# Layer 1's 8-bit product moved by tiles into its attention, and wider products for the absorbed weights

## The chip, the core and the metric

The kernel runs on one core of a Trainium2 chip. The metric is the device time of one execution in microseconds (us), as a median over several runs. The core has a matrix engine (TensorE, PE in the profile; PEld is its loading of the stationary operand), VectorE (DVE), ScalarE (ACT), GpSimd (POOL), and SyncE (SP), which here only issues transfers (DMAs). Each engine executes its own instructions in order and waits for the others through semaphores. PE writes its products to PSUM; DVE and ACT copy them from there to SBUF.

## The reference, cut to what matters

Four layers over x (16 sequences of 56 tokens, width 256), each an attention over a context of 1500 positions and a feed-forward part. Layers 1 to 3 have a latent attention with 16 heads; layers 0, 2 and 3 end in experts with a router, layer 1 in one product with 8-bit weights and inputs that are rounded to 8 bits.

```python
# attention of layers 1 to 3 (layer 2 also ropes q_big)
q_hk = (hidden_q @ Wq.T).reshape(b, s, H, K)
q_big = einsum('bshk,hkq->bshq', q_hk, w_kc_q)
q_r = einsum('bshq,hqr->bhsr', q_big, W_qr)
k_r = einsum('bld,hdr->bhlr', kv_rope, W_kr)
attn = softmax(einsum('bhsr,bhlr->bhsl', q_r, k_r))
ctx_c = einsum('bhsl,bld->bhsd', attn, kv_rope)
ctx_lat = einsum('bhsd,hkd->bshk', ctx_c, w_kc_kv)
out = ctx_lat.reshape(b, s, H * K) @ Wo.T
# feed-forward part of layer 1
w = weight.astype(f32) * weight_scale
x_fp8 = clip(x / input_scale, -448, 448).astype(float8_e4m3fn)
out = einsum('bsi,oi->bso', x_fp8.astype(f32) * input_scale, w)
# each layer
x = x + tanh(g_xattn[l]) * attention(layernorm(x))
x = x + tanh(g_ffn[l]) * feed_forward(layernorm(x))
```

## The kernel before

The tokens stay in SBUF as eight tiles of 112 rows (`x`, two sequences each). Instructions are traced in the order of the Python code; a scheduler may move them on their engine, except that `in_order` pins an instruction behind the one traced before it on the same engine. Nearly all of the steps here are pinned, the queries (L346, L337) are not.

**Absorbing.** The weights of the latent attention do not depend on tokens, so for each group `g` of two heads `absorbing` multiplies them into two matrices: `M`, which turns a normalized token into the two heads' queries against the latent context, and `G`, which turns the heads' contexts into the output. Layers 1 and 3 have three products in a chain, with a copy out of PSUM behind each: W_qr times W_kr (L280, `e`), w_kc_q times `e` (L288, `f`), Wq times `f` (L297, `M`), and w_kc_kv times Wo (L304, `G`). Layer 2 ropes between, so it keeps two factors: `M` of 384 columns (L258, L259) and `er` (L265, copied by L267 and, under a mask by `C_H`, by L269). `load_heads` fetches a group's six weights over SP's queue (L231), two buffers to a weight. Some groups are absorbed ahead of a layer (`Next.absorb`; several at once take turns), the others within `queries`.

**Queries.** For layers 1 and 3, `queries` computes all queries of a group in two halves of 448 tokens (L337), and `spread` copies each with DVE (L316) and ACT (L318); the next group's absorption is traced between. Layer 2 has three products (L346), the roping (L350, L353, and L354 on POOL), and two products more (L360, L362).

**Attention.** `attention_mla` goes through 56 steps, seven to a tile of tokens, each 128 queries of two sequences. In loop turn `k`, step `k` gets its scores (PE, L711), maxima (DVE, L723 to L728) and exponentials (ACT, L734, L743), step `k - 1` has its probabilities turned (PE, L773) and copied (DVE L776, ACT L778), and step `k - 2` multiplies them with the context (PE, L785) and keeps the result (DVE, L796). The sums of the exponentials are inverted and go through memory to all partitions (`invert`, SP, L760 and L762). In layer 1 the next tile's keys are turned in three of the steps (L696). When a tile's seven steps are done, `project(t)` multiplies its contexts by `G` (L808) and adds to `x` (L810), as a generator of which `next(after)` traces one part at a time, at three places of each turn: one behind the first maxima, two behind the exponentials. In layers 2 and 3 the router's work on that tile follows in the same generator (L922 to L1015).

**The 8-bit product.** `fp8_matrix` loads the 8-bit weights (three DMAs on SP) and decodes them on DVE by integer operations (L1450 to L1464), between layer 1's queries and its attention. `fp8_linear` runs behind the attention, with two tiles at a time: statistics, ACT's square root (L172), normalizing, rounding to 8 bits in float32 (L1479 to L1485), turning (L189, L190), two products to a tile (L1494), the addition to `x` (L1499), then the normalization of the result and its turning to `xnT`, the input of layer 2's queries. Four absorptions of layer 2 are traced in between.

The main program's order for layer 1:

```python
    with tc.tile_pool(name="f1w", bufs=1, reuse_waits="tile") as keep:
        matrix = []
        attention_mla(1, nxt, behind_queries=lambda: matrix.extend(fp8_matrix(keep)))
        nxt.whole.close()
        nxt = Next(2)
        fp8_linear(*matrix, nxt)
```

## Time and profile before

| | us |
|---|---|
| median of 3 runs | 2435.41 |
| lowest and highest run | 2428.84, 2443.81 |
| profiled execution | 2433.22 |
| its span, of which the profile's times are told | 2431.4 |

Where the span goes, by stretches of the trace:

| stretch (us from the start) | what | PE busy | granted PE clock |
|---|---|---|---|
| 0 to 310.5 | layer 0 | 244.4 | 0.87 |
| 310.5 to 338 | two absorptions of layer 1, layer 0's sums | 25.9 | 0.72 |
| 338 to 391 | layer 1's queries | 48.7 | 0.97 |
| 394.5 to 914.5 | layer 1's attention | 513.9 | 0.98 |
| 914.5 to 955.6 | the 8-bit product, four absorptions of layer 2 | 33.0 | 0.75 |
| 955.6 to 1076 | layer 2's queries | 117.2 | 1.00 |
| 1076 to 1598 | layer 2's attention | 512.8 | 0.99 |
| 1598 to 1688 | layer 2's experts, three absorptions of layer 3 | 80.3 | 0.83 |
| 1688 to 1736 | layer 3's queries | 45.0 | 1.00 |
| 1736 to 2258 | layer 3's attention | 515.0 | 0.99 |
| 2258 to 2431 | layer 3's experts, output | 135.6 | 0.93 |

How to read the profile: its page gives busy times and, in 40 slices of the span, tenths of each engine's busy share and of the PE clock that was granted. A row of the timeline has the start, the duration, the engine, the line of the kernel, the operation, output and inputs by the program's names, and in brackets how long the engine stood idle before it and what ended that. Rows of a window table have the stretch, its length, each engine's busy time with its number of instructions, then the granted clock, the DMA engines' busy share and GB/s. A row of waits has the waiting engine and line, what it waited for, the total, how often, and the longest. A float32 product appears as two records on PE, a transpose as one.

### The profile page before, as it was taken

How to read it: one execution, taken by the hardware profiler on the slowest of the kernel's cores; microseconds unless marked ns; L12 is line 12 of the kernel's file. 1: busy time of each engine (PE TensorE's matmuls, PEld its weight loads, DVE VectorE, ACT ScalarE, POOL GpSimd, SP SyncE). 2: the span in 40 equal slices, each digit the busy share in tenths (PEclk: the TensorE clock that was granted, in tenths of full speed). 3: DMA queues.
4: the chain of work that ended last, by engine and by line, in shares of the span. 5: the costliest groups of instructions: out<-in, count | busy, mean ns of one | idle time of the engine just before them, and what ended most of it. 6: DMA issues, size and time to landing. Idle time of an engine off the chain costs nothing. (4 is left out here: it accounts for less than half of the span.)

```text
span 2431.4 us, 48119 instructions
## 1 busy us (share of the span) xinstructions
PE 2273.1 (93%) x18034; PEld 1648.4 (68%) x18034; DVE 1507.5 (62%) x3384; ACT 1234.8 (51%) x2705; POOL 411.8 (17%) x707
## 2 busy tenths in 40 slices
PE   8678988999999998989999999979899999999687
PEld 5445665777777776447777777755577777777454
DVE  4752335667666667767777777724477777777222
ACT  4312325666666662346666666612566666665231
POOL 4454810000000001430000000001001111111223
PEclk9769988999999998999999999989899999999899
DMA  7736742000000002100000000045200000000497
GB/s 215 220 97 183 222 132 75 22 22 22 21 21 22 22 23 61 35 28 22 22 24 23 24 24 23 11 153 166 61 22 16 27 26 28 28 29 17 151 282 207
DMA packets 114115, 171.93 MB, mean 71 GB/s; under 512 B 20154, under 2 KB 75971, under 8 KB 112852
## 3 DMA queue, kind: packets, MB, share of 16 engines
q1 hardware_dynamic: 104342, 150.30, 20.4%
q0 software_dynamic: 7600, 17.14, 2.2%
q8 instruction: 145, 2.38, 0.4%
q10 hardware_dynamic: 1934, 1.34, 0.2%
q14 instruction: 94, 0.77, 0.1%
HBM read 130.19 MB, written 40.48 MB: 70 GB/s over the span
## 5 line engine op out<-in xcount | busy, mean ns | idle before, releaser
L734 ACT ACTIVATE p<-s_ps,nm 128x500 f32<-128x500 f32 x504 | 335.7, 675 | 396.8 <-DVE nm L725 396.8
L723 DVE TENSOR_REDUCE part<-s_ps 128x1 f32<-128x500 f32 x504 | 340.5, 677 | 262.9 <-PE s_ps L711 262.7
L711 PE MATMUL s_ps<-kvT,qT 64*128 64x500 f32 x2016 | 484.4, 607 | 13.7 <-ACT p L734 6.3
L785 PEld LDWEIGHTS m_ps<-pT,kv 125*64 125x64 f32 x8064 | 436.7, 137 | 76.7 <-issue 69.5
L785 PE MATMUL m_ps<-pT,kv 125*64 125x128 f32 x8064 | 477.3, 275 | 2.2 <-ACT pT L778 1.7
L711 PEld LDWEIGHTS s_ps<-kvT,qT 64*128 64x128 f32 x2016 | 185.5, 189 | 198.4 <-issue 121.1
L773 PE MATMUL m_ps<-ident,p 128*125 128x128 f32 x2016 | 299.4, 283 | 0.3
L728 DVE TENSOR_REDUCE nm<-s_ps 128x1 f32<-128x1500 f32 x168 | 287.1, 1709 | 2.3 <-PE s_ps L711 2.3
L773 PEld LDWEIGHTS m_ps<-ident,p 128*125 128x125 f32 x2016 | 249.4, 188 | 36.5 <-issue 27.0
L743 ACT ACTIVATE p<-s_ps,nm 128x1500 f32<-128x1500 f32 x168 | 254.9, 1517 | 1.3 <-DVE nm L728 0.8
L773 PE MATMUL s_ps<-ident,p 128*125 128x128 f32 x2016 | 251.3, 275 | 0.0
L754 POOL TENSOR_TENSOR den<-den 128x1 f32<-128x1 f32 x168 | 33.4, 199 | 1217.7 <-ACT p L734 1217.4
L773 PEld LDWEIGHTS s_ps<-ident,p 128*125 128x125 f32 x2016 | 237.1, 190 | 0.0
L778 ACT COPY pT<-s_ps 125x512 f32<-125x512 f32 x336 | 181.2, 598 | 90.6 <-PE s_ps L773 76.7
L778 ACT COPY pT<-m_ps 125x512 f32<-125x512 f32 x336 | 185.7, 620 | 0.0
L1217 PE MATMUL gu_ps<-wgu,xT 128*128 128x448 f32 (+2 forms) x344 | 144.0, 546 | 21.2 <-DMA wgu<-in_L_wgu 14.7
L796 DVE TENSOR_TENSOR ctxT<-m_ps,rep 64x128 f32<-64x128 f32 (+1 forms) x384 | 104.4, 272 | 88.4 <-PE m_ps L785 81.6
L1222 DVE TENSOR_TENSOR act<-gu_ps,act 128x224 f32<-128x224 f32 (+2 forms) x78 | 31.2, 400 | 193.3 <-ACT act L1221 193.3
L318 ACT COPY qT<-q_ps 64x224 f32<-64x224 f32 x128 | 71.8, 561 | 109.3 <-PE q_ps L362 71.0
L776 DVE COPY pT<-m_ps 125x512 f32<-125x512 f32 x168 | 116.2, 691 | 10.0 <-PE s_ps L773 0.4
L776 DVE COPY pT<-s_ps 125x512 f32<-125x512 f32 x168 | 114.3, 680 | 0.0
L1217 PEld LDWEIGHTS gu_ps<-wgu,xT 128*128 128x128 f32 x344 | 63.9, 195 | 72.3 <-issue 31.4
(289 smaller groups left out, 2651.2 us busy)
## 6 DMA issues: line engine op xcount, KB each, us to landing
wgu<-in_L_wgu SPq DMA_DIRECT2D x36, 448.0 KB
rows<-zero SPq DMA_DIRECT2D x16, 899.5 KB
kvT<-turned_kv SPq DMA_DIRECT2D x16, 750.0 KB
wgu<-in_L_wgu SPq DMA_DIRECT2D x34, 352.0 KB
rep<-through SPq DMA_DIRECT2D x336, 32.0 KB
xrow<-rows SPq DMA_DIRECT2D x78, 128.5 KB
wgu<-in_L_wgu SPq DMA_DIRECT2D x8, 1024.0 KB
wd<-in_L_wd SPq DMA_DIRECT2D x36, 224.0 KB
```

The lines of the kernel that those rows point to most:

```text
L318: nc.scalar.copy(o, i)
L711: in_order(nc.tensor.matmul(o[:, 0 : 4 * KP], qT[64 * b : 64 * b + 64, t, j * QT : (j + 1) * QT], kvTs[t][64 * b : 64 * b + 64, z * 4 * KP ...
L723: in_order(nc.vector.tensor_reduce(self.part[:, z : z + 1], sp0[z][:, 0 : 4 * KP], AX.X, ALU.max))
L728: in_order(nc.vector.tensor_reduce(self.nm[1], sp1[:, :, 0 : 4 * KP], AX.XY, ALU.max, negate=True))
L734: in_order(nc.scalar.activation(self.p[0][:, 4 * z * KP : 4 * (z + 1) * KP], sp0[z][:, 0 : 4 * KP], AF.Exp, bias=self.nm[0], accum_out=sel ...
L743: in_order(nc.scalar.activation(self.p[1].rearrange("p (z c) -> p z c", z=3), sp1[:, :, 0 : 4 * KP], AF.Exp, bias=self.nm[1], accum_out=se ...
L773: in_order(nc.tensor.transpose(ps[:, c, :], self.p[b][:, k : k + KP], ident))
L776: in_order(nc.vector.tensor_copy(o, ps))
L778: in_order(nc.scalar.copy(o, ps))
L785: in_order(nc.tensor.matmul(self.pv[64 * b : 64 * b + 64, :], kv[:, self.t, c, b, :], self.pT[:, c, b, :], start=c == 0, stop=c == KC - 1))
L796: in_order(nc.vector.tensor_tensor(ctxs[self.t][64 * a : 64 * a + 64, b, lo - 448 * a : hi - 448 * a], self.pv[64 * b : 64 * b + 64, cols] ...
L1217: in_order(nc.tensor.matmul(ps[:, s, 0:n], xT[:, k, :], wgu[:, k, s * n : (s + 1) * n], start=k == 0, stop=k == 1))
```

## The change

The decoding becomes a generator of 14 parts; from the second turn on, two are traced at the end of each turn of layer 1's attention, the three loads with the first. `fp8_linear` becomes `fp8_tile`, for one tile, which continues `project(t)` as the router does in layers 2 and 3; a fourth `next(after)` stands at the end of each turn, behind DVE's copies. Its roots are Newton steps on DVE (`inverse_root`) where ACT's square root stood, and its turned tiles and products use the two shared PSUM banks (`misc`). The last tile's parts are what is left behind the loop: they are traced around layer 2's absorptions, taken two at a time.

In `absorbing`, layer 2 multiplies Wq by all 192 columns at once and copies `M` in two pieces; its second factor is two products over 128 rows, with the weights laid out in blocks and the mask in the weights. Layers 1 and 3 multiply in another order: W_qr with w_kc_q first, two heads in two column halves of the array, then one product over 128 rows with W_kr in diagonal blocks. The weights are laid out for this on the host, so `wqr` and `wkr` are larger.

```diff
-        room = {"wkc": 512}.get(name, size)
-        w = wpool.tile([128 if name == "wkc" else p, room], F32, tag=name, name=name)[0:p, 0:size]
+        room = {"wkc": 512, "wqr": 256}.get(name, size)
+        w = wpool.tile([128, room], F32, tag=name, name=name)[0:p, 0:size]
         w = w.rearrange("p (n a) -> p n a", n=n) if len(rest) == 1 else w.rearrange("p (n a c) -> p n a c", n=n, a=rest[0])
...
             M = pool.tile([128, 2, 3 * 128], F32, name="Mr", bufs=bufs)
             for k in range(2):
-                ps = misc()
+                ps = misc()[:, 0 : 2 * DQ].rearrange("p (j c) -> p j c", j=2)
                 for j in range(2):
-                    lhsT = wq[:, j, k * 128 : (k + 1) * 128]
-                    rest = ps[:, 256:384].rearrange("p (b j c) -> p j b c", b=2, j=2)[:, j]
-                    pin(nc.tensor.matmul(ps[:, j * 128 : (j + 1) * 128], lhsT, wkc[:, j, 0:128], start=True, stop=True))
-                    pin(nc.tensor.matmul(rest, lhsT, wkc[:, j, 128:192].rearrange("p (b c) -> p b c", b=2), start=True, stop=True))
-                pin(nc.scalar.copy(M[:, k, :], ps[:, 0:384]))
+                    pin(nc.tensor.matmul(ps[:, j, :], wq[:, j, k * 128 : (k + 1) * 128], wkc[:, j, :], start=True, stop=True))
+                pin(nc.scalar.copy(M[:, k, 0:256].rearrange("p (j c) -> p j c", j=2), ps[:, :, 0:128]))
+                rest = M[:, k, 256:384].rearrange("p (b j c) -> p j b c", b=2, j=2)
+                pin(nc.scalar.copy(rest, ps[:, :, 128:DQ].rearrange("p j (b c) -> p j b c", b=2)))
                 yield
             ps = misc()
-            for j in range(2):
-                for lhsT, o in ((wqr[:, j, :], 0), (wqr[:, 2, :], 128)):
-                    pin(nc.tensor.matmul(ps[:, o + j * DC : o + (j + 1) * DC], lhsT, wkr[:, j, :], start=True, stop=True))
+            for i in range(2):
+                pin(nc.tensor.matmul(ps[:, i * 128 : (i + 1) * 128], wqr[:, 0, i, :], wkr[:, 0, :], start=True, stop=True))
             e = pool.tile([128, 2, 128], F32, name="er", bufs=bufs)
-            pin(nc.scalar.copy(e[:, 0, :], ps[:, 0:128]))
-            for j in range(2):
-                pin(nc.scalar.activation(
-                    e[:, 1, j * DC : (j + 1) * DC], ps[:, 128 + j * DC : 128 + (j + 1) * DC], AF.Copy, scale=small[:, C_H + j : C_H + j + 1]
-                ))
+            pin(nc.scalar.copy(e.rearrange("p i c -> p (i c)"), ps[:, 0:256]))
             yield
             made[g] = M, e
         else:
             ps = misc()
-            for j in range(2):
-                for i in range(2):
-                    c = (2 * j + i) * DC
-                    pin(nc.tensor.matmul(ps[0:96, c : c + DC], wqr[:, j, i * 96 : (i + 1) * 96], wkr[:, j, :], start=True, stop=True))
-            e = pool.tile([96, 2, 2, DC], F32, name="e")
-            pin(nc.scalar.copy(e.rearrange("p j i c -> p (j i c)"), ps[0:96, 0 : 4 * DC]))
+            for i in range(2):
+                for j in range(2):
+                    pin(nc.tensor.matmul(
+                        ps[64 * j : 64 * j + 64, 0:128], wqr[:, j, i, :], wkc[:, j, i, :], start=i == 0, stop=i == 1, skip_group_check=True
+                    ))
+            e = pool.tile([128, 128], F32, name="e")
+            pin(nc.scalar.copy(e, ps[:, 0:128]))
             yield
             ps = misc()
-            for j in range(2):
-                for i in range(2):
-                    pin(nc.tensor.matmul(ps[:, j * DC : (j + 1) * DC], wkc[:, j, i, :], e[:, j, i, :], start=i == 0, stop=i == 1))
+            pin(nc.tensor.matmul(ps[:, 0 : 2 * DC], e, wkr[:, 0, :], start=True, stop=True))
             f = pool.tile([128, 2, DC], F32, name="f")
             pin(nc.vector.tensor_copy(f.rearrange("p j c -> p (j c)"), ps[:, 0 : 2 * DC]))
...
-    def attention_mla(l, nxt, router=None, behind_queries=None):
+    def attention_mla(l, nxt, router=None, behind=None, tail=None):
...
             nxt.stack.close()
-            if behind_queries:
-                behind_queries()
             for g in range(2 if l < 3 else 0):
                 load_absorbed(l + 1, g)
...
                 if router is not None:
                     yield from router.token_tile(t)
+                if tail is not None:
+                    yield from tail(t)
...
                         turn.turned(i)
+                if tail is not None:
+                    if k > 0:
+                        next(behind, None)
+                        next(behind, None)
+                    next(after, None)
                 if val and val.j == nq - 1:
                     for _ in after:
                         pass
                     after = project(val.t)
-            for _ in after:
-                pass
+            if tail is None:
+                for _ in after:
+                    pass
+            else:
+                next(after)
+                next(after)
+            return after
...
-    def fp8_matrix(keep):
-        w8 = keep.tile([128, 2, D], F32, name="w8")
-        sc = keep.tile([128, 4], F32, name="sc")
+    def fp8_matrix(w8, sc):
...
-            nc.vector.tensor_copy(wi, wb)
-            nc.vector.tensor_scalar(mag, wi, 0x7F, None, ALU.bitwise_and)
...
+            in_order(nc.vector.tensor_copy(wi, wb))
+            yield
+            in_order(nc.vector.tensor_scalar(mag, wi, 0x7F, None, ALU.bitwise_and))
+            yield
...
-            nc.vector.tensor_tensor(sc[:, 3:4], sc[:, 0:1], sc[:, 1:2], ALU.mult)
-            nc.vector.tensor_tensor(sc[:, 3:4], sc[:, 3:4], gates[:, 5:6], ALU.mult)
-        return w8, sc
-    def fp8_linear(w8, sc, nxt):
...
-            for t in range(0, NT, 2):
-                normed.stats(t)
-                normed.stats(t + 1)
-                normed.root(t)
-            nxt.absorb(0, 1)
-            for t in range(0, NT + 4, 2):
-                if t < NT:
-                    quantize(t)
-                    multiply(t)
-                if t in (2, 4):
-                    nxt.absorb(t // 2 + 1)
-                if 2 <= t < NT + 2:
-                    add(t - 2)
-                    nxt.normed.stats(t - 2)
-                    nxt.normed.stats(t - 1)
-                    nxt.normed.root(t - 2)
-                if t >= 4:
-                    nxt.normed.apply(t - 4)
-                    nxt.normed.turn(t - 4)
...
+            in_order(nc.vector.tensor_tensor(sc[:, 3:4], sc[:, 0:1], sc[:, 1:2], ALU.mult))
+            yield
+            in_order(nc.vector.tensor_tensor(sc[:, 3:4], sc[:, 3:4], gates[:, 5:6], ALU.mult))
+            yield
+    def fp8_tile(t, w8, sc, pool):
+        def stats():
+            st = pool.tile([TP, 6], F32, name="st")
+            mv = pool.tile([TP, 2], F32, name="mv")
+            in_order(nc.vector.bn_stats(st, x[:, t, :]))
+            in_order(nc.vector.bn_aggr(mv, st))
+            return mv
+        def apply(mv, rstd):
+            v = pool.tile([TP, D], F32, name="xn")
+            in_order(nc.vector.tensor_scalar(v, x[:, t, :], mv[:, 0:1], rstd, ALU.subtract, ALU.mult))
+            return v
+        def turn(v, o):
+            ps = misc()[:, 0 : 2 * TP].rearrange("p (k c) -> p k c", k=2)
+            for k in range(2):
+                in_order(nc.tensor.transpose(ps[:, k, :], v[:, k * 128 : (k + 1) * 128], ident[0:TP, 0:TP]))
+            in_order(nc.scalar.copy(o, ps))
+        yield
+        mv = stats()
+        rstd = yield from inverse_root(pool, mv[:, 1:2])
+        yield
+        v = apply(mv, rstd)
+        c = pool.tile([TP, D], F32, name="c8")
+        in_order(nc.vector.tensor_scalar(v, v, sc[0:TP, 2:3], None, ALU.mult))
+        in_order(nc.vector.tensor_scalar(v, v, 448.0, -448.0, ALU.min, ALU.max))
+        for _ in range(4):
+            yield
+        in_order(nc.vector.tensor_scalar(c.bitcast(I32), v.bitcast(I32), 0x7F800000, None, ALU.bitwise_and))
+        in_order(nc.vector.tensor_scalar(c, c, 2.0**-6, 1.5 * 2.0**20, ALU.max, ALU.mult))
+        in_order(nc.vector.tensor_tensor(v, v, c, ALU.add))
+        in_order(nc.vector.tensor_tensor(v, v, c, ALU.subtract))
+        yield
+        x8 = pool.tile([128, 2, TP], F32, name="x8T")
+        turn(v, x8)
+        for _ in range(4):
+            yield
+        ps = misc()[0:TP, 0:D]
+        for k in range(2):
+            in_order(nc.tensor.matmul(ps, x8[:, k, :], w8[:, k, :], start=k == 0, stop=k == 1))
+        yield
+        in_order(nc.vector.scalar_tensor_tensor(x[:, t, :], ps, sc[0:TP, 3:4], x[:, t, :], ALU.mult, ALU.add))
+        yield
+        yield
+        mv = stats()
+        rstd = yield from inverse_root(pool, mv[:, 1:2])
+        yield
+        v = apply(mv, rstd)
+        yield
+        turn(v, xnT[:, :, t, :])
...
-    with tc.tile_pool(name="f1w", bufs=1, reuse_waits="tile") as keep:
-        matrix = []
-        attention_mla(1, nxt, behind_queries=lambda: matrix.extend(fp8_matrix(keep)))
+    with ExitStack() as keep:
+        f1w = keep.enter_context(tc.tile_pool(name="f1w", bufs=1, reuse_waits="tile"))
+        matrix = f1w.tile([128, 2, D], F32, name="w8"), f1w.tile([128, 4], F32, name="sc")
+        parts8 = keep.enter_context(tc.tile_pool(name="f1c", bufs=1, reuse_waits="tile"))
+        left = attention_mla(1, nxt, behind=fp8_matrix(*matrix), tail=lambda t: fp8_tile(t, *matrix, parts8))
         nxt.whole.close()
         nxt = Next(2)
-        fp8_linear(*matrix, nxt)
+        nxt.absorb(0, 1)
+        for _ in range(14):
+            next(left)
+        nxt.absorb(2, 3)
+        for _ in left:
+            pass
...
-        wqr = i[p + "W_qr"].transpose(2, 0, 1)
+        wqr = i[p + "W_qr"]
         if l == 2:
-            wqr = wqr[:, :, order].reshape(64, 8, 2, DQ)
-            rest = wqr[..., 128:].reshape(64, 8, 2, 2, 32).transpose(0, 1, 3, 2, 4).reshape(64, 8, 1, 128)
-            wqr = np.concatenate([wqr[..., 0:128], rest], axis=2).reshape(64, 24, 128)
-        a[f"L{l}_wqr"] = wqr
-        a[f"L{l}_wkr"] = i[p + "W_kr"].transpose(2, 0, 1)
+            wqr = wqr[:, order, :].reshape(8, 2, DQ, 64).transpose(1, 3, 0, 2)
+            both = np.zeros((2, 64, 8, 2, 128), np.float32)
+            both[:, :, :, 0, :] = wqr[..., 0:128]
+            for j in range(2):
+                both[j, :, :, 1, :].reshape(64, 8, 2, 2, 32)[:, :, :, j, :] = wqr[j, ..., 128:].reshape(64, 8, 2, 32)
+            a[f"L{l}_wqr"] = both.reshape(128, 8, 2, 128)
+        else:
+            a[f"L{l}_wqr"] = wqr.reshape(H, 2, 96, 64).transpose(2, 0, 1, 3)
+        blocks = np.zeros((2, 64, 8, 2, 64), np.float32)
+        for j in range(2):
+            blocks[j, :, :, j, :] = i[p + "W_kr"].reshape(8, 2, 64, 64)[:, j].transpose(2, 0, 1)
+        a[f"L{l}_wkr"] = blocks.reshape(128, 8, 128)
```

## The prediction, made before the change was run

> **What bounds the kernel now.** I read the page first (shares, slices), then layer 1 in stretches, then one step of its attention in order of time, then the waits of the stretch behind it, then one group of the queries.
>
> ```profile
> PE 2273.1 (93%) x18034; PEld 1648.4 (68%) x18034; DVE 1507.5 (62%) x3384; ACT 1234.8 (51%) x2705; POOL 411.8 (17%) x707
> PEclk9769988999999998999999999989899999999899
> ```
>
> TensorE (PE) is busy 93% of the span, so a PE instruction counts unless PE is idle or slow there. Layer 1 by stretches (engine busy times, then granted clock):
>
> ```profile
> 415.00:900.00 485.00, 485.00 (x4731) 376.56 (x4730) 332.63 (x615) 309.91 (x669) 21.05 (x108) 1.00 0.06 20
> 914.50:921.20 6.70, 2.15 (x19) 1.98 (x18) 5.82 (x24) 1.26 (x6) 0.00 (x0) 0.90 0.00 0
> 921.20:931.00 9.80, 9.80 (x44) 8.20 (x44) 7.27 (x16) 3.38 (x11) 0.00 (x0) 0.50 0.22 64
> 931.00:944.00 13.00, 10.88 (x55) 8.11 (x54) 8.29 (x25) 3.62 (x10) 0.00 (x0) 0.76 0.33 103
> 944.00:955.60 11.60, 10.12 (x56) 7.92 (x56) 8.80 (x26) 3.63 (x11) 0.17 (x1) 0.87 0.48 146
> ```
>
> The attention (first row) has PE busy throughout, VectorE (DVE) 69%, ScalarE (ACT) 64%. The 8-bit product and the first absorptions of layer 2 (41.1 us, 914.5 to 955.6) have PE idle or at half clock. One step of the attention:
>
> ```profile
> 875.95 2.79 PE L711 MATMUL s_ps<-kvT,qT 64*128 64x500 f32 x12
> 877.09 0.68 DVE L723 TENSOR_REDUCE part<-s_ps 128x1 f32<-128x500 f32 x1 [1.42 <-PE s_ps L711]
> 878.66 2.84 PE L785 MATMUL m_ps<-pT,kv 125*64 125x128 f32 x48
> 879.73 0.68 ACT L734 ACTIVATE p<-s_ps,nm 128x500 f32<-128x500 f32 x1 [2.78 <-DVE nm L725]
> 881.43 0.70 PE L773 MATMUL m_ps<-ident,p 128*125 128x128 f32 x4
> 884.25 2.79 PE L711 MATMUL s_ps<-kvT,qT 64*128 64x500 f32 x12
> ```
>
> A step is 8.30 us (875.95 to 884.25) and PE sets it: scores, values, transposes follow each other without a hole, while DVE waits 1.42 before the next maxima and ACT 2.78. With the keys' transposes and the output projection, seven steps (a tile) take 63.4. What PE waited for behind the attention:
>
> ```profile
> PEld m_ps L258 <- ACT Mr L260: 4.7, 1, 4.7
> PEld o_ps L1494 <- ACT x8T L190: 3.7, 4, 1.0
> PEld m_ps L189 <- ACT er L269: 1.3, 2, 0.6
> ```
>
> The 4.7 is a copy that stood behind four square roots in ACT's order, each waiting for DVE's statistics. In layer 1's queries, a group with its absorption:
>
> ```profile
> 380.11 0.89 PE L280 MATMUL m_ps<-wkr,wqr 64*96 64x64 f32 x8
> 382.53 1.00 PE L288 MATMUL m_ps<-e,wkc 96*128 96x64 f32 x8
> ```
>
> These groups start every 6.53 us (373.57, 380.11), and PE fills that.
>
> **Part 1: the product moves into the attention.** Per tile PE gains 4 transposes (as 2 + 2) and 2 products of 256 columns (a product is two records, a transpose one). The nearest rows are in layer 2's loop, where the router does the same kind of thing: its step with two transposes (L935) is 8.64 instead of 8.30, so 0.34 each time. For the product: 16 records of the projection (L808, 256 columns) lengthen a step by 3.75, that is 0.214 a record and 0.33 around them; four records 0.85 + 0.3 = 1.15. A tile: 0.34 + 1.15 + 0.34 = 1.83; seven tiles in the loop: **+12.8**.
>
> Against this stands a rule of the Trainium skill ("TensorEngine Tiling (Array Packing)", Key Properties): a change of tiling mode drains TensorE. The loop alternates 64-row, 64-column and full shapes, and every part adds a full-shape stretch between the first two. The trace's price: a step's records at their own spacing are 2.50 + 2.57 + 2.57 = 7.64, so its three changes cost 0.66, 0.22 each, and a stretch put between costs 0.15 (transposes) to 0.33. If each of the 21 stretches paid two drains of one transpose's length (0.28), the loop would cost 0.56 x 21 + (0.19 + 0.85 + 0.19) x 7 = 20.4. I take the trace's, and keep 20 as the far end.
>
> DVE gains 33 instructions a tile: statistics 2 x 0.61, two Newton roots of 2.1 (1596.08 to 1598.18 in layer 2's tail), two normalizations 0.41, scaling to rounding about 2.0 (half the width of L1479 to L1485, whose six take 3.2), the addition 0.48: 8.8 us, against 31% of 63.4 = 20 free. What sits in the fourth slot lies in the 1.42 before the next maxima; the longest, statistics with half a root, is 1.8 and is 0.4 late, which the next two maxima (0.16 idle before each) nearly win back. The rest of a root (0.9) falls in slot three, before the context copies; the router's, with a normalization behind it, costs its step 0.29; I take **+0.7** over the loop, 0 to 4. ACT's two copies (L937: 0.35) lie in its 2.78. The shared PSUM pair gets three more tenants a tile, each emptied before its turn comes round.
>
> **Part 2: decoding.** Its ten wide DVE operations (0.42 to 0.68) stand now among the first step's maxima (393.8 to 403.9). Gone from there, the first exponentials come about 1.9 earlier; PE is at half clock then, I take -1.3. Its three DMAs went out on SP at 385, ahead of the twelve weight loads; they now stand behind these and behind step 1's four denominator transfers, which wait for each other until 417.3. The first DVE part (a cast) waits in order for a load that lands about 1.5 later, near 419, with step 2's maxima (416.5 before) behind it, their exponentials behind those and PE's transposes behind these: about 2.8 late at the exponentials, 1.0 to 1.4 of it hidden: +1.8. Sum **+0.5** (-2 to +3). POOL's queue issues nothing new.
>
> **Part 3: the stretch left behind.** From 914.5 PE keeps four absorptions and tile 7's share. An absorption is 3.85 at full clock (938.64 to 942.5); wider (part 4) about 2.7, so 10.8; tile 7 1.6; waits: DVE needs some 5.5 for tile 7 (from 915.4), covered by two absorptions (5.4 + copies); then groups 2 and 3 need their weights. SP issues these when group 0's tiles come free, now about 918 (before 926.8), and the DMA busy row of before shows both groups in about 10 after the first issue: late 927 to 928. PE could idle 2 to 3 there, unless layer 2's first queries, whose tokens are ready, fill in. I take 2. So queries start in effect near 914.5 + 10.8 + 1.6 + 2 = 928.9 instead of 955.6; 1.7 of transposes among them (L189, 957 to 960) go too, and about 1.4 of DVE's work for tile 7 comes in: **-27** (-20 to -31). Tile 7's second half (4 us of DVE) is needed only at the queries' second half, 25 us on.
>
> The stretch 944 to 955.6 shows a clock of 0.87 although no wait behind the 4.7 is over 1.0. The skill's rule ("TensorE: Matmul & The Clock Gate", Part 1: the clock gate) says that it takes an idle window of about 3.4 us to put the array at half clock. By the rule waits of 2 to 3 leave the 10.8 as they are; by the row they would be 10.8 / 0.87 = 12.4, and after a long wait, as in the row of 0.50, up to ten us at half speed, +5. PE has fewer holes now than it had there (1.5 in 11.6), so I take the rule's, and keep +5.
>
> **Part 4: wider products.** Records of 448 columns come every 0.375, so 0.84 ns a column: 192 columns 0.16, 128 columns 0.107.
> Layers 1 and 3: L288's eight records (1.00) become two (0.21); L280's (0.75 to 0.89) become eight of 128 columns in two column halves, 0.43 to 0.86 (L785's halves run side by side). About -0.8 a group where PE is the limit, which it is while DVE's and ACT's alternating copies (2.33 a half, 4.66 a group) stay below 5.7: 11 groups in the queries, I take **-8** (0 to -11).
> Outside them: two groups at 310.6 to 322.3 at half clock, ahead of the sums over loads that begin to land near 318: -2.5; one at 1611 to 1618.5, -1; two at 1670.8 to 1679.6, -1.5; together **-5** (0 to -8).
> Layer 2, four groups in the queries: L258/L259 2.0 to 1.3, L265 0.96 to 0.43, but M takes two ACT copies for one (0.37 + 0.3 for 0.48) and PE already waits for them (0.91 before L265): **-1.2** (0 to -3.6). The new weight tiles are larger (wqr 96 to 128 KB, wkr 32 to 64), 0.3 us of a group's transfer, counted in part 3.
>
> **The sum:** 12.8 + 0.7 + 0.5 - 27 - 8 - 5 - 1.2 = -27. The profiled execution is 2433.2 (span 2431.4), so 2406; it lies 2.2 under the median of the runs, 2435.4, for which I say **2408**.
>
> **Rivals.** *The gain is covered* (0.30): absorptions 2 and 3 wait for their weights past 3.4 us and run cold (-20), and the queries prove bound by the alternating copies (-3 in place of -8, -2 outside): 14 - 20 - 3 - 2 = -11, 2424. For it: DVE and ACT hand over to each other in 1.2 us waits there; against: DVE waits 1.70 for PE once a group.
> *The loop turns into DVE's* (0.06), the slower side: the chain maxima, exponentials, transposes has about 1.0 to spare per step. If slot parts push it over, for instance a copy out of PSUM queued behind exponentials while both shared banks are held, PE stops in nearly every of the 49 steps. From 27 / 49 = 0.55 a step the gain is gone; as the chain's whole spare and 0.2 on top, 1.2 a step, it is 59 more, -27 + 59 = +32, 2467. Against it: the router's parts in layers 2 and 3, of the same size, lengthen a tile by 1.6 (63.46 against 61.85), no more.
> *It does not do what it says* (0.08): the scheduler leaves layer 2's queries behind tile 7's whole chain (1.6 of PE, 9 of DVE and ACT in series), so -27 becomes -18 and the layer is even: about -16 with part 4, 2419.
> Mine: 0.56, itself 2397 to 2417.
>
> **Numbers.** A measurement here tells about 1% (24 us) from no change. Under 2411: most of mine (0.50) and a little of the others: 0.53. Slower by over 1%: 0.06. The rest, 0.41, lies within. The range 2394 to 2427 holds all of mine but its far ends, and the two covered cases.
>
> **What would show it.** Plain steps of layer 1 stay 8.30; three steps a tile grow by 0.34, 1.15, 0.34; step 2 has DVE waiting for the 8-bit weights. Layer 2's first L346 starts before 933 with the clock at 1.00. L280 starts every 5.7 us in the queries. I am wrong if a plain step is over 8.6, if PE waits over 3.4 for weights near 922, or if the query groups keep 6.5.

## The result and the profile after

The changed kernel took 2395.4 us (median of 4 runs, 2385.2 to 2398.7) beside 2432.1 for the kernel before on the same chip (4 runs, 2428.8 to 2443.8): a ratio of 0.984, interval 0.980 to 0.988. Its profiled execution took 2395.7 (span 2393.6), 37.5 less than the profiled execution of before. The forecast's sum was 27 less, 2408 for the median: the measured time lies in its wide range (2394 to 2427), but below the 2397 to 2417 of the account that it argued for. The direction and the largest term held. What was sized wrong is the clock.

First the two lines of the page that answer to those shown of before: busy times, and the granted clock by slices.

```profile
PE 2244.0 (94%) x17842; PEld 1611.7 (67%) x17842; DVE 1531.0 (64%) x3552; ACT 1231.9 (51%) x2703; POOL 411.6 (17%) x707
PEclk9769989999999999989999999999899999999899
```

PE is busy 29 us less and DVE 24 us more. That is mostly the Newton roots: their two costliest lines (L137, L141) took 23.9 us before and take 44.9 now. Now stretches of the changed kernel (engine busy times, granted clock, DMA share, GB/s): the same 485 us of layer 1's attention, then what stands behind it.

```profile
409.00:894.00 485.00, 485.00 (x4649) 374.22 (x4647) 376.48 (x833) 308.75 (x663) 20.28 (x104) 1.00 0.06 20
...
914.00:921.00 7.00, 7.00 (x38) 4.46 (x36) 5.84 (x21) 3.28 (x11) 0.00 (x0) 1.00 0.25 71
921.00:933.00 12.00, 12.00 (x54) 7.38 (x53) 7.97 (x14) 4.22 (x14) 4.54 (x4) 1.00 0.56 177
933.00:945.00 12.00, 12.00 (x39) 5.32 (x38) 11.38 (x28) 3.93 (x9) 5.10 (x5) 1.00 0.35 114
```

DVE went from 333 to 376 in the attention, and PE still has no hole there. The stretches behind it, which had PE at 2.15 of 6.70 us and then at clocks of 0.50 to 0.87, now have it full at 1.00. In order of time on PE, from the end of the last projection:

```profile
914.06 3.20 PE L256 MATMUL m_ps<-wkc,wq 128*128 128x192 f32 x16
917.10 0.70 PE L264 MATMUL m_ps<-wkr,wqr 128*128 128x128 f32 x4
917.64 0.92 PE L340 MATMUL big_ps<-xnT,Mr 128*128 128x448 f32 x2
...
921.04 0.41 PE L1504 MATMUL m_ps<-ident,xn 112*128 112x112 f32 x2
921.30 1.68 PE L340 MATMUL big_ps<-xnT,Mr 128*128 128x448 f32 x4
922.82 0.81 PE L256 MATMUL m_ps<-wkc,wq 128*128 128x192 f32 x4
923.47 3.17 PE L340 MATMUL big_ps<-xnT,Mr 128*128 128x448 f32 x8
926.47 2.37 PE L256 MATMUL m_ps<-wkc,wq 128*128 128x192 f32 x12
...
932.53 1.12 PE L1529 MATMUL m_ps<-w,x8T 128*112 128x256 f32 x4
```

L256 and L264 are absorptions, L340 layer 2's queries. Queries stand between the absorptions from 917.64 on: they fill both the time until groups 2 and 3 have their weights (transfers keep the DMA engines busy until about 926, and queries run from 923.47 to 926.47) and the waits of tile 7's chain, whose product (L1529) comes at 932.53. Tiles are numbered from 0, so tile 7 is the last.

By stretches of the span, each of two profiles of each kernel (the second ones are experiments below), with the forecast's terms sorted into the same stretches ("last score" is where the last step's scores start):

| stretch (us) | before | changed | difference of the first ones | forecast |
|---|---|---|---|---|
| start to layer 1's first absorption (code not touched) | 310.6, 310.7 | 309.4, 305.2 | -1.1 | 0 |
| to layer 1's first query | 27.65, 26.89 | 23.62, 24.09 | -4.0 | -2.5 |
| queries of layers 1 and 3 | 103.9, 104.0 | 98.4, 96.8 | -5.5 | -8 |
| layer 1's attention, first two steps | 20.85, 20.69 | 15.65, 17.28 | -5.2 | -1.3 |
| third step to last score | 477.18, 477.19 | 488.02, 488.09 | +10.8 | +15.3 |
| to layer 2's first score | 183.6, 183.1 | 154.7, 155.5 | -28.9 | -28.2 |
| layer 2's last score to layer 3's first query | 117.2, 117.3 | 110.9, 108.0 | -6.2 | -2.5 |
| all the rest | 1190.5, 1192.1 | 1192.8, 1186.1 | +2.3 | 0 |

### The profile page after: what moved, and what is told of

It is laid out like the page before. It is cut to its first block, busy times and chain, and to the rows that moved or that the text cites. A ratio compares the mean times of both kernels' runs of the same rounds, so it can differ in the third digit from the quotient of the medians.

```text
span 2393.6 us, 47915 instructions
## 1 busy us (share of the span) xinstructions
PE 2244.0 (94%) x17842; PEld 1611.7 (67%) x17842; DVE 1531.0 (64%) x3552; ACT 1231.9 (51%) x2703; POOL 411.6 (17%) x707
```

## The experiments

Times are medians of four runs where nothing else is said, ratios those to the kernel before on the same chip with their intervals. The kernel before differs by up to 7 us from chip to chip, so kernels that ran on different chips are compared by ratio or by stretch. "Cold" means that the granted clock is half.

**One part at a time.** First the wider products alone, then the move alone:

```diff
 # the kernel before, and of the change only
-                    pin(nc.tensor.matmul(ps[:, j * 128 : (j + 1) * 128], lhsT, wkc[:, j, 0:128], start=True, stop=True))
+                    pin(nc.tensor.matmul(ps[:, j, :], wq[:, j, k * 128 : (k + 1) * 128], wkc[:, j, :], start=True, stop=True))
...
```

> The kernel before with the wider absorption products alone; the 8-bit product stays behind the attention, its decoding ahead of it. If the gains that the two profiles show in places with nothing but absorption and queries belong to the products (pair at the end of layer 0 and what follows -4, layer 1's queries -2.6, layer 3's pair with the experts around it -4 to -5, its queries -3, layer 2's queries -1), the profiled execution is about 15 us under the 2433 of before, near 2418. Rival: what lies outside the queries is drift of the granted clock and not the products; then only the queries' 6 to 7 are left, near 2426. As I forecast the terms (-8, -5, -1.2) it is -14.

Measured: 2407.9, ratio 0.991 (0.988 to 0.993); the profile's span is 26.8 under before.

```diff
 # the changed kernel, with absorbing() and its weights' layout as before
-            pin(nc.tensor.matmul(ps[:, 0 : 2 * DC], e, wkr[:, 0, :], start=True, stop=True))
+            for j in range(2):
+                for i in range(2):
+                    pin(nc.tensor.matmul(ps[:, j * DC : (j + 1) * DC], wkc[:, j, i, :], e[:, j, i, :], start=i == 0, stop=i == 1))
...
```

> The changed kernel with the old, narrow absorption products: the 8-bit product in the loop, the decoding in the loop. By the profiles: first tile -5, six further tiles +1.7 each and the last +0.7, stretch and layer 2's queries -30, of which about 4 x 1.1 = 4.5 are the narrower absorptions; together about -20, near 2413. By the terms of my forecast (+14 for the loop with its start, -27 with narrower absorptions -22.5) it would be -8.5, near 2425. If the parts are independent, this run's gain and that of the products alone add up to the 37 of the whole change.

Measured: 2413.6, ratio 0.993 (0.990 to 0.996); the stretch behind the attention is 159.2. So 0.9 and 0.7% lie in the parts, 1.6 in the whole: they add up within the intervals. One stretch is shared. Behind the attention the products alone bring 8.3 (183.6 to 175.3), but on top of the move only 4.4 (159.2 to 154.7): the half clock there, 20.5 us in the kernel before, is 7.8 with the products alone and none with the move alone, so the move had taken it away already. The products alone brought more than the 15 us that I had read from the two traces: the 8.3 had not been in that reading, and 2.6 each came from layer 1's first two steps (18.24 with the decoding still in front of them) and from the untouched first 310 us.

**The decoding, put back in front.**

```diff
             nxt.stack.close()
+            for _ in behind or ():
+                pass
...
-                    if k > 0:
-                        next(behind, None)
-                        next(behind, None)
```

> The changed kernel with the decoding back between the queries and the attention; the tiles' parts stay in the loop. Theory: the ten wide operations among the first step's maxima are what made the first tile 64 us long, through a wait of TensorE above 3 us behind which the clock is halved for over 10 us; with them back the first tile is again about 64 (59.0 without), the transposes of the first step run at half clock, and the time is 4.5 to 5.5 longer than the changed kernel's, near 2401. Rival: their direct delay only, as I forecast it (1.3): near 2397, with the first tile at 60 to 61, the rest of its gain being another start state of the clock behind the shorter queries.

Measured: 2394.5, ratio 0.985 (0.982 to 0.988): no difference in the time. In the profile the first step is 7.97 as in the kernel before (4.54 and 6.16 in the two of the changed kernel) and the first two are 18.75. The first tile is 62.0, between theory and rival; this run decides nothing, because places of the same size with holes come out 2 to 3 us apart between runs. It was taken up again below.

**The transposes next to other full-shape work.**

```diff
         in_order(nc.vector.tensor_tensor(v, v, c, ALU.subtract))
-        yield
+        for _ in range(4):
+            yield
         x8 = pool.tile([128, 2, TP], F32, name="x8T")
         turn(v, x8)
-        for _ in range(4):
-            yield
+        yield
...
         v = apply(mv, rstd)
-        yield
+        for _ in range(4):
+            yield
         turn(v, xnT[:, :, t, :])
```

> The changed kernel with both pairs of transposes of a tile three places later: behind the transposes of the probabilities, ahead of the next scores, so that no stretch of full shape is put between scores and values. If a stretch costs its records (0.19) and about 0.15 for the change of shape, two steps a tile grow by 0.2 in place of 0.34: some 2 us less over the loop, about 2394. If each stretch pays two drains (0.56), it is 7 to 8 us less. Rival: no gain, since transposes stand now ahead of scores that PE could start at once, and since their copies stand in ScalarE's order ahead of the exponentials: steps grow as before or by more, 2396 to 2400.

Measured: 2402.1, ratio 0.987 (0.985 to 0.989). Steps with a pair grow by 0.90, not 0.34, more than even the rival said, and third step to last score is 495.2. The first two steps, whose code is that of the changed kernel, are 18.86 here. PE in order of time, in this kernel:

```profile
501.49 1.04 PE L765 MATMUL m_ps<-ident,p 128*125 128x128 f32 x8
503.01 0.41 PE L1504 MATMUL m_ps<-ident,xn 112*128 112x112 f32 x2 [0.49 <-ACT pT L770]
503.35 2.79 PE L703 MATMUL s_ps<-kvT,qT 64*128 64x500 f32 x12
```

and in the changed kernel:

```profile
881.79 2.79 PE L703 MATMUL s_ps<-kvT,qT 64*128 64x500 f32 x12
884.50 0.41 PE L1504 MATMUL m_ps<-ident,xn 112*128 112x112 f32 x2
884.85 2.84 PE L777 MATMUL m_ps<-pT,kv 125*64 125x128 f32 x48
```

The pair of shared banks sets the price of the place: right behind the probabilities' transposes both are still being copied out, so the transposes wait 0.49; between scores and values one is free. The other 0.41 is no less than 0.34, so standing next to full-shape work saved nothing: neither my 0.15 for the change of shape nor the 0.56 for two drains shows.

**The same kernel again.**

> The changed kernel once more, for a second profile and more times. In all six profiles so far the half-clock stretches begin and end on a grid of 3.413 us whose phase differs from run to run. Theory: how many of its windows turn cold at the few places with short holes is chance, so this profile repeats the changed kernel's steady rows to the hundredth (tile 65.13, query groups, 488.0 from layer 1's third step to its last) but not the places with holes: the first two steps of layer 1's attention come out anywhere from 15.6 to 19, the stretch from layer 3's first absorption to its pair anywhere from 55 to 60. Rival: these belong to the program, then they repeat to 0.3 us (15.65 and 55.45). Time by either 2390 to 2400.

Measured: 2386.9, ratio 0.983 (0.980 to 0.985). Steady rows repeat (65.13 a tile, 488.09). The first two steps came to 17.28. Layer 3 has one absorption ahead of a pair of them: from the first to the pair took 54.4 in place of 55.45, and from there to the layer's first query 13.9 in place of 16.6. So single places do vary, by 1 to 3 us, though not over the span that I had allowed.

> The kernel before once more, for a second profile. Steady rows repeat (477.2 from layer 1's third step to its last, query groups 6.53, 27.6 from the first absorption to layer 1's first query). If the first two steps of layer 1 with the decoding ahead of them are near 18.5 here (as in the two kernels with it in front, 18.24 and 18.75), then 20.85 was a bad draw of the clock grid and the decoding's move is worth some 1.5 to 2.5 us; if they are near 20.9 again, the start is worth 3 to 5. The same for the 59.6 from layer 3's first absorption to its pair: about 55 if it was chance, 60 if it belongs to this kernel.

Measured: 2433.9 in a single run. The first two steps are 20.69 again, and layer 3's first absorption to its pair takes 59.71, so neither was a rare draw of the kernel before. How much of the gain at the start is the decoding's does not follow from this: the wider products alone had 18.24 with the decoding in front, and the run with moved transposes had 18.86 without it.

**Filled starts.** The second step's scores are put in another order, and `occupy(n)` multiplies ones with ones `n` times, 512 columns each, to keep TensorE busy.

```diff
-                        new.scores(z)
+                        new.scores(z, (0,) if k == 1 else (0, 1))
                         new.maxima0(z)
+                    for z in range(3 if k == 1 else 0):
+                        new.scores(z, (1,))
...
+                if k == 0:
+                    occupy(6)
```

> The changed kernel with the start of all three later attentions filled: the second step's scores go first to the three banks that come free early and then to the wide one, and six 512-column products of ones stand between the first two steps. Theory: holes of 1 to 3.7 us at this place are what half the clock; without them the first two steps, 15.65, 18.75 and 20.34 us in layers 1, 2 and 3, come to 12 to 14 each, and the time falls by 8 to 14, to 2382 to 2388. Rival: the cold windows come from the holes at the end of the queries, ahead of the first score; then each start gains the reordering only, about 1 us, 2392 to 2394.

Measured: 2378.6, ratio 0.980 (0.976 to 0.983). The three starts are 15.10, 18.27 and 16.45: shorter, not the 12 to 14 expected. The half-clock stretch that is left begins 0.2 to 1.5 us behind the holes that end the queries at each of them, so here the rival was half right.

**The holes ahead of the starts filled too.** On top of the filled starts:

> The kernel with the filled starts, and the holes ahead of them filled too: the third keys' transposes of layer 1 go to a free score bank in place of the shared pair (a wait of 2.0), nine products of ones ahead of layer 2's last turned queries (a wait of 2.5), four ahead of layer 3's first scores (waits of 0.6 and 1.2). Over nine profiles a grid window in which TensorE was busy for less than half was followed by a cold one in about nine of ten cases, one with over 70% in 1 of 100. If that is the cause, no cold window follows at the three starts, the first two steps come to 11 to 13 us each (15.1, 18.3, 16.5 with filled starts alone), and the time falls by 6 to 10 under the filled starts' 2378, to 2368 to 2372. Rival: the products of ones delay the queries or the first scores as much as they save: 2376 to 2380.

```diff
             if before:
+                occupy(9)
                 project_turned(*before)
...
-                ps = misc()
+                ps = sp0[2] if (t, z) == (0, 2) else misc()
...
+            if l == 3:
+                occupy(4)
```

Measured: 2386.0 on a chip with 2434.9 for the kernel before, ratio 0.981 (0.976 to 0.985). The starts are 13.41, 15.01 and 14.68, without one cold window among them: the mechanism held, though they are longer than the 11 to 13 expected. The time I gave did not hold: the ratio is that of the filled starts alone. From layer 1's first absorption to the last score of layer 3 it takes 1873.5, the filled starts alone 1877.2, the changed kernel 1885.8 and 1883.0; the untouched work around it gave it back in this run (311.5 in front, 199.8 at the end).

> The kernel with filled starts and filled holes ahead of them once more, on the same chip as the run with the decoding in front. The three starts repeat without a cold window (first two steps 13.4, 15.0, 14.7 us, each within 0.5), which they would not if their warmth had been a draw of the grid's phase; time between 0.978 and 0.982 of the kernel before.

Measured: 2378.8, ratio 0.981 (0.978 to 0.983); 13.42, 15.02, 14.68. The starts repeat to the hundredth.

**The decoding in front, where nothing else is cold.** The last kernel with the edit of the decoding in front.

> The kernel with filled starts and filled holes ahead of them (first two steps of layer 1 13.41 us, no cold window there), with the decoding put back between queries and attention. What the decoding costs by itself, apart from the clock: by my forecast its ten wide operations delay the first exponentials by 1.9 and TensorE by about 1.3, so the first two steps come to 14.7 if TensorE stays warm. Theory: they also open a hole of over 2 us behind the first scores, longer than the products of ones fill, a window under half busy follows and a cold one behind it, so they come to 16 to 18. Rival: nothing, the decoding fits beside the products of ones: 13.4 to 13.8.

Measured: 2386.0, ratio 0.983 (0.980 to 0.986), and 19.28 us for the first two steps in place of 13.41, more than the theory's 16 to 18. PE in order of time, first with the decoding in the loop:

```profile
388.25 2.79 PE L705 MATMUL s_ps<-kvT,qT 64*128 64x500 f32 x12 [1.58 <-ACT kvT L692]
390.97 1.47 PE L119 MATMUL m_ps<-onesb 128*128 128x512 bf16 x6
392.80 5.59 PE L705 MATMUL s_ps<-kvT,qT 64*128 64x500 f32 x12 [0.35 <-ACT p L728]
398.31 0.70 PE L767 MATMUL m_ps<-ident,p 128*125 128x128 f32 x4
```

and with it in front:

```profile
383.67 2.79 PE L707 MATMUL s_ps<-kvT,qT 64*128 64x500 f32 x12 [1.58 <-ACT kvT L694]
386.39 1.47 PE L119 MATMUL m_ps<-onesb 128*128 128x512 bf16 x6
390.71 8.17 PE L707 MATMUL s_ps<-kvT,qT 64*128 64x500 f32 x12 [2.85 <-ACT p L730]
398.81 1.22 PE L769 MATMUL m_ps<-ident,p 128*125 128x128 f32 x4
```

The hole in front of the second scores grows by 2.5 (0.35 to 2.85). A cold stretch of 10.2 us follows it, in which the same twelve records take 8.17 in place of 5.59 and the transposes 1.22 in place of 0.70. So of the 5.9 that the first two steps grow, the operations cost 2.5 by themselves; the other 3.4 go with the cold stretch (these records alone are 3.1 longer).

**The loop without the tail's work on TensorE.**

```diff
-        turn(v, x8)
+        in_order(nc.scalar.copy(x8[0:TP], v.rearrange("p (k c) -> p k c", k=2)[:, :, 0:TP]))
...
-        for k in range(2):
-            in_order(nc.tensor.matmul(ps, x8[:, k, :], w8[:, k, :], start=k == 0, stop=k == 1))
...
```

> The changed kernel without the tail's work on TensorE: its transposes and products are left out, ScalarE copies the normalized tile instead, VectorE does all its parts (the output is not the reference's). If the loop's price is TensorE's own work, as I forecast, a tile of layer 1 is 63.4 again, and from the third step to the last 477.2 in place of 488.0. If VectorE's parts hold up the maxima, some of the 1.73 a tile stays: a step with statistics and half a root or one with the rest of a root shows 8.4 to 8.7.

Measured in a single run: 63.4 a tile, all steps 8.30 where nothing else of PE's stands in them, third step to last score 477.45: of the loop's 10.8, PE's own records and what surrounds them are 10.6 and DVE's parts 0.3. (Behind layer 1 other tokens go to other experts in this kernel, so its full time says nothing.)

**Tile 7's rest all in front of the absorptions.**

```diff
+        for _ in left:
+            pass
         nxt.absorb(0, 1)
-        for _ in range(14):
-            next(left)
         nxt.absorb(2, 3)
-        for _ in left:
-            pass
```

> The changed kernel with the last tile's leftover parts all ahead of layer 2's four first absorptions, in order on each engine. TensorE then has in its order two transposes that wait for some 5.5 us of VectorE, two products, two transposes that wait for another 4, and only then the absorptions; nothing else is ready for it. Theory: the wait of about 8 to 9 us is paid in full and cold windows follow, so from the last score of layer 1 to layer 2's first it is 10 to 14 us longer than the changed kernel's 154.7, and the time 2405 to 2410. Rival: layer 2's queries on the first seven tiles need the absorptions, but the wait hides something that was waiting anyway (weights of groups 2 and 3, 4 us): then only 4 to 6.

Measured: 2400.6, ratio 0.988 (0.986 to 0.991); 168.7 behind the attention, 14.0 more than the 154.7. PE in order of time:

```profile
908.36 3.79 PE L800 MATMUL m_ps<-G,ctxT 128*112 128x256 f32 x16 [0.80 <-DVE ctxT L788]
918.28 0.64 PE L1504 MATMUL m_ps<-ident,xn 112*128 112x112 f32 x2 [6.13 <-DVE xn L1521]
919.35 2.05 PE L1529 MATMUL m_ps<-w,x8T 128*112 128x256 f32 x4 [0.43 <-ACT x8T L1505]
925.33 0.61 PE L1504 MATMUL m_ps<-ident,xn 112*128 112x112 f32 x2 [3.93 <-DVE xn L1498]
925.73 4.53 PE L256 MATMUL m_ps<-wkc,wq 128*128 128x192 f32 x16
```

DVE's chain for one tile stands open: 10.5 us of waits (6.13 + 0.43 + 3.93), and then the absorptions' first 16 records take 4.53 in place of 3.20. So what hides this in the changed kernel are the absorptions and queries between these parts.

## Which step of the forecast failed, and which held

By the profiled executions the gain was 10.6 us larger than forecast, and 9.1 of that lie in two terms with one fault: I priced what was taken away under a granted clock that stays as it was. The first two steps (-1.3, measured -5.2) and the wider products outside the queries (-5, measured -10.2) were sized as work and waits at half clock, while in the runs fewer windows are at half clock once that work is gone. The errors of the other terms nearly cancel. In order:

**The loop (12.8 + 0.7): mechanism right, size near.** Plain steps stayed 8.30, PE set every step. Pairs of transposes cost the 0.34 taken from the router's steps; the product's step grew by 1.05, not 1.15. A tile is 1.73 longer, not 1.83 + 0.1. Priced by two drains a stretch, after the Trainium skill's rule on changes of tiling mode ("TensorEngine Tiling (Array Packing)", Key Properties), the loop would have been 20.4 longer. Of the forecast's seven whole tiles the last one's product and second pair (1.4) fall behind the last score, so 10.8 in the loop is 12.2 in the forecast's count. DVE's 33 operations a tile cost 0.3 over the loop, where I took 0.7. The rival in which the loop turns into DVE's is out.

**The wait for the 8-bit weights (1.8): did not come.** VectorE in order of time, at the first decoding parts:

```profile
402.90 0.39 DVE L1454 CAST wi<-wb 128x512 int32<-128x512 uint8 x1
403.32 0.43 DVE L1456 TENSOR_SCALAR mag<-wi 128x512 int32<-128x512 int32 x1
403.67 1.41 DVE L715 TENSOR_REDUCE part<-s_ps 128x1 f32<-128x500 f32 x2
```

The cast starts without a wait and maxima follow at once; the third step is 8.97 and 9.04 against 8.88. I had put the load behind the denominators' transfers in SP's queue, where it stands in the Python code. The queue itself, in order of time, has it ahead of them by 6.7 us (why, was not looked into):

```profile
387.89 0.39 SPq L1446 DMA_DIRECT2D wb<-in_L_w  x1
...
394.61 1.19 SPq L752 DMA_DIRECT2D through<-rd  x2
```

**The first two steps (-1.3): the step that failed.** The changed kernel's are 5.2 and 3.4 shorter. I had said "PE is at half clock then" and priced the operations' removal under a clock that stays. But those operations lengthen the hole that stands ahead of the cold windows: before, in PE's order of time,

```profile
394.52 4.28 PE L711 MATMUL s_ps<-kvT,qT 64*128 64x500 f32 x12
402.49 2.03 PE L711 MATMUL s_ps<-kvT,qT 64*128 64x500 f32 x2 [3.69 <-ACT p L734]
405.30 5.36 PE L711 MATMUL s_ps<-kvT,qT 64*128 64x500 f32 x10 [0.78 <-ACT p L743]
410.60 1.22 PE L773 MATMUL m_ps<-ident,p 128*125 128x128 f32 x4
```

and after,

```profile
386.76 2.79 PE L703 MATMUL s_ps<-kvT,qT 64*128 64x500 f32 x12
391.31 1.67 PE L703 MATMUL s_ps<-kvT,qT 64*128 64x500 f32 x2 [1.75 <-ACT p L726]
394.12 4.95 PE L703 MATMUL s_ps<-kvT,qT 64*128 64x500 f32 x10 [1.14 <-ACT p L735]
399.00 0.70 PE L765 MATMUL m_ps<-ident,p 128*125 128x128 f32 x4
```

The wait falls from 3.69 to 1.75, half clock ends at 398.5 in place of 414.6 (6.8 us of it in these two steps, before 16.7), and the transposes are at 0.70 again. With all other holes filled, the decoding's place is worth 5.9 (19.28 against 13.41), shown by taking only it back.

In the kernels without filled holes the size is in part a draw. Six profiles without the decoding in front, whose code for these two steps is the same, have 14.87, 15.65, 17.11, 17.28, 17.36 and 18.86; four with it have 18.24, 18.75, 20.69 and 20.85. The means differ by 2.8, so about half of the 5.2 is luck. (The two longest are the kernel before, the only one that has the narrow products as well, so a part may be theirs.) What separates the profiles is mostly the half clock in these steps, 3.4 to 13.7 us of it in the six and 10.2 to 16.7 in the four. Where it is about 10 in both, three without (17.1 to 17.4) are some 1.3 shorter than two with (18.2 and 18.8): the forecast's -1.3, which left out only that the operations also change how much of the stretch is cold.

**Wider products outside the queries (-5): the same mistake, and here beyond the scatter.** They brought 4.0 and 6.2 (2.8 and 9.2 in the second profiles). From layer 2's last score to layer 3's first query the ten profiles with wide products (all but the one whose tokens go elsewhere) take 107.6 to 114.0, the three with narrow ones 117.2 to 120.2. I had taken the saved records' own time at half clock. The shorter absorptions also leave fewer cold windows to the experts and queries around them. This stretch, before and after (the granted clock is the third figure from the end):

```profile
1571.70:1688.90 117.20, 102.36 (x560) 69.47 (x560) 39.53 (x126) 27.24 (x61) 11.61 (x17) 0.87 0.48 166
...
1541.10:1652.00 110.90, 95.15 (x541) 63.00 (x541) 39.45 (x126) 27.03 (x61) 11.60 (x17) 0.92 0.50 176
```

Half clock falls from 30.7 us to 17.1. The products alone have 23.9 there, the move alone 34.1, so it is the products and not the move. That they do it through the clock is read from these thirteen profiles, not from a run that holds the clock fixed.

**In the queries (-8): a little too much.** Layer 3's take 47.6 with narrow and 44.7 to 44.9 with wide products in every profile. Layer 1's fall from 56.3 to 53.7, in the second profiles from 56.4 to 52.1; two windows of the first changed profile are cold there, one in each of the others. A group of the changed kernel, in order of time:

```profile
355.59 0.66 PE L274 MATMUL m_ps<-wkc,wqr 96*64 96x128 f32 x8
...
357.78 0.46 PE L282 MATMUL m_ps<-wkr,e 128*128 128x128 f32 x2
...
361.45 0.66 PE L274 MATMUL m_ps<-wkc,wqr 96*64 96x128 f32 x8
```

The period is 5.86, where I forecast 5.7: the first product shrank as said (0.89 to 0.66), the second to 0.46 and not to 0.21, and the period is that of PE's records, which follow each other without a hole.

**Behind the attention (-27 and -1.2): right**, 28.9 with the 1.4 of tile 6, the seventh, inside. Layer 2's first query came at 917.64, "before 933", and the clock stayed full until 1043.7, so the 5 us kept in reserve for a cold stretch were not needed. The rival with groups 2 and 3 cold is out: their weights came late, as it said, but queries stood in the hole. The rival that leaves queries behind tile 7's chain describes the kernel with tile 7 in front; it costs 14, more than the 9 I gave it. (The sum of that rival is also off: by its own terms the change would have brought 18, not 16.)

**The sum.** Against 27 forecast: 4.5 more from the loop (1.8 of it the wait that did not come, and 1.4 only counted elsewhere), 3.9 from the start, 5.2 from the absorptions outside, 2.5 less from the queries, and 0.5 less from everything else: some 37.7, where the profiled executions differ by 37.5. The median came 12.6 under the forecast, at the low end of the range. The two places where I held the clock constant make 9.1 of the difference, of which some 2.4 is the draw at the start (5.2 against 2.8).

A version that beats both kernels: with filled starts the ratio is 0.980 (0.976 to 0.983), twice 0.981 with the holes ahead filled too, the changed kernel's 0.984 and 0.983. By time alone the intervals overlap; by the stretch between layer 1's first absorption and layer 3's last score it is 6 to 17 us ahead.

## What to carry to other kernels

Price a removed operation under the clock that will hold without it: in these runs a hole of 2 to 4 us on TensorE cost its length and then often up to ten us at half speed behind it, so look at the holes ahead of every cold stretch before giving a size to what stands in it. And do not size such a place from one profile of each kernel: the same code took 14.9 to 18.9 us. When parts are threaded into a tight loop, ask which shared bank is free at the place, not which neighbour has the same shape: two transposes cost 0.34 in one gap and 0.90 in the other. And a chain on a slower engine is hidden only by what stands between its parts in the order; put in one piece it cost its full 10.5 us and a cold clock.

## What the runs showed of the hardware

The half-clock stretches lie on a grid. In each of the fourteen profiles they begin and end on multiples of 3.413 us, with a phase that differs from run to run. The Trainium skill ("TensorE: Matmul & The Clock Gate", Part 1: the clock gate) gives a free-running window of 3413 ns, which agrees; its advice, to avoid idle gaps of more than about 3.4 us, does not go far enough here. Counting TensorE's busy share (matmuls and weight loads together) in each window of these profiles from the first clock record on, and what clock the next window had:

```text
window at full clock, busy share    windows   next one at half clock
under 10%                                38    38
10 to 50%                               156   143
50 to 60%                                92    31
60 to 70%                               115    11
70 to 90%                               708     4
over 90%                               7930     2
window at half clock
under 80%                               296   296
over 80%                                392   163
```

Half a window of holes was mostly enough to halve the clock: the 2.85 us above did it, and with filled starts the 2.00 ahead of layer 1's first scores. Once cold, no window that was under 80% busy brought the clock back, and of those over 80% a little more than half did. It fits this that untouched code scatters, since the same holes fall differently into the windows: the first 310 us, alike in all these kernels, took 304.5 to 311.5. Not explained are three cold windows of the kernel before: from 943.7 to 947.1 (the row with the clock 0.87), where the window ahead was 78% busy by the records, and, in both of its profiles, in the middle of layer 3's pair of absorptions (from 1674.2 in the first), where the window ahead was 97 and 99% busy. In all three many of the records ahead use part of the array's rows or columns; whether such records count less was not tried.
